# Second layer: the product of decay and state in an SBUF tile of its own, a later input between product and sum, and TensorE's spread of inputs ahead of most decays

## Chip, cores and metric

The kernel runs on one core of a Trainium2 chip. The metric is the device time of one execution, in microseconds (us), from a few executions of the same program. Everything is float32. Engines are named as in the profile: PE (TensorE; PEld are its weight loads), DVE (VectorE), ACT (ScalarE), POOL (GpSimd), SP (SyncE, which issues the DMAs). An instruction that is said to wait stands in its engine's queue, and everything behind it in that queue waits too.

## What is computed

Sixteen images of 128 x 56 x 56 go through two layers. Layer 0 (a depthwise convolution, window attention with routing, a depthwise 5 x 5 convolution and an MLP) isn't touched by the change. Layer 1 is a 3 x 3 convolution, a small state-space scan over eight tokens of 16 channels for every pixel, a group norm, a SiLU and a residual. The change is in the scan:

```
dA = jnp.exp(dt[..., None] * A)
dBx = dt[..., None] * Bm[:, :, None, :] * xc[..., None]

def step(h, inp):
    a, b, c = inp
    h = a * h + b
    return (h, jnp.sum(h * c[:, None, :], axis=-1))
```

The state h has 32 x 16 elements for each of 16 x 56 x 56 sequences, and eight tokens l = 0 to 7 follow each other.

## The kernel before

Layer 0 runs first, image by image; layer 1 follows from about 3.2 ms on and takes the rest. Its work is cut into 112 groups (16 images, seven blocks of 448 pixels each). A group goes through 14 steps, k = 0 to 13, in the loop at the end of `layer1` (L1284). A state of one token is a tile of 128 partitions x 4 x 448 elements; each step treats one half of it (`jp` = 0 or 1, two of the four slices, 896 elements per partition), so that two steps make one token, and the token of step k is l = 1 + k // 2.

Each engine runs its instructions in the order of the program text: `_chain` ties every instruction of the stage to the one before it on the same engine. What a step issues, in this order:

- `advance` (DVE): the product of decay and former state for step k. For l < 7 it is written in place over the decay in PSUM (L1001); for l = 7, whose input is accounted for elsewhere, it goes straight to the state's tile (L999).
- other DVE parts of the step (for k > 0): `collect` at k = 3 and 12 (L1032), `statistics` at k = 9 and 10 (L1080).
- `complete` (DVE, L1006): the sum of the product and the input, written to the state's tile in SBUF. It exists for l < 7, that is in steps 0 to 11.
- `inject` (DVE, L991): the input of step k + 4, made from the spread input in PSUM and a broadcast gate, written to the tile of its state. It takes that tile from the tag `h`, which has four buffers.
- at k = 0 only, `direct_mul` (DVE, L960), two instructions.
- `decay` (PE, L973) for step k + 2: two small matmuls into a PSUM tile of the tag `a`, which has two buffers.
- `spread` (PE, L984) for step k + 5: two small matmuls into the PSUM tile `x`, which has one buffer.
- `decay_exp` (ACT, L976): the exponential of the decay, in place in PSUM.
- `weigh` (POOL, L1010) in odd steps: the whole state of a token times a gate, 1792 elements per partition, into `cst`.
- further PE and POOL parts of the step from `work` (L1153): on PE the sums over weighted states (`gather`, L1019), the convolution of the next image, projections and transposes; on POOL `gated` (L1035) at k = 4 and 13, `rate_sum` (L922 to L925, four instructions) at k = 6 and 8, `product` (L951) at k = 10, and `store` (L1126) at k = 2 in four of seven groups.

SP brings the gates of the groups by DMA and stores the results. DVE's sum and weighing are joined by a semaphore: `weigh` of a token waits for the `complete` of its second half. The sum also waits on a semaphore for the product in front of it, on its own engine.

Of the kernel before, what the change touches and what calls it, by code (L numbers as in the profile page):

```python
# [10 lines left out]
F32 = mybir.dt.float32  # L11
U32 = mybir.dt.uint32
AF = mybir.ActivationFunctionType
ALU = mybir.AluOpType
# [3 lines left out]
P = 128  # L18
# [5 lines left out]
BLK = 448  # L24
# [771 lines left out]
def layer1(ctx: ExitStack, tc: tile.TileContext, x1, t, out, conv):  # L796
# [15 lines left out]
    nc = tc.nc  # L812
# [3 lines left out]
    cst = ctx.enter_context(tc.tile_pool(name="l1c", bufs=1))  # L816
    w1 = ctx.enter_context(tc.tile_pool(name="l1w1", bufs=1))
    w2 = ctx.enter_context(tc.tile_pool(name="l1w2", bufs=2))
# [14 lines left out]
    vec = conv.vec  # L833
# [5 lines left out]


    for w, name in ((wx, "b_kx"), (wv, "b_dtw")):
        k = w1.tile(list(w.shape), F32, tag="fold", name=name)
        nc.sync.dma_start(k, t[name])
        nc.vector.tensor_mul(w, w, k)
    nc.scalar.activation(adec, adec, AF.Exp)
    nc.vector.scalar_tensor_tensor(adec, adec, -1.0, mask, ALU.mult, ALU.mult)
    dd = cst.tile([P, P], F32, tag="dd", name="dd")
    nc.vector.tensor_scalar_mul(dd, ident, d_w)
    eps = cst.tile([P, 1], F32, tag="eps1", name="eps1")
    nc.vector.memset(eps, GN_EPS)  # L850
    neg = cst.tile([P, 1], F32, tag="neg", name="neg")
    nc.vector.memset(neg, -1.0)

    y, tails = conv.y, conv.tails
    pq = [ps_q.tile([P, 512], F32, tag=f"q{k}", name=f"pq{k}") for k in range(2)]
# [11 lines left out]
    def own(jp):  # L867
        return slice(2 * jp, 2 * jp + 2)
# [86 lines left out]
        nc.tensor.matmul(pq[0][:, 0:BLK], lhsT=cbm, rhs=p["cb"], start=True, stop=True)  # L955

    def direct_mul(p):
        ud = p["ud"] = w2.tile([P, 2, BLK], F32, tag="ud", name=f"ud_{p['n']}")
        for h in range(2):
            nc.vector.scalar_tensor_tensor(  # L960
                ud[:, h, :], pq[0][:, 0:BLK], vec[:, 6 + h : 7 + h], p["dtx"][:, h, :], ALU.mult, ALU.mult
            )


# [3 lines left out]
    def decay(p, l, jp):  # L968
        h, l4 = divmod(l, 4)
        a = p["a", l, jp] = ps_a.tile([P, 2, 512], F32, tag="a", name=f"a_{p['n']}_{l}_{jp}")[:, :, 0:BLK]  # L970
        for k in range(2):
            rows = slice(32 * (2 * jp + k), 32 * (2 * jp + k) + 32)
            nc.tensor.matmul(a[:, k, :], lhsT=adec[rows, l4, :], rhs=p["dt"][rows, h, :], start=True, stop=True)  # L973

    def decay_exp(p, l, jp):
        nc.scalar.activation(p["a", l, jp], p["a", l, jp], AF.Exp)  # L976

    def spread(p, l, jp):

        h, l4 = divmod(l, 4)  # L980
        x = ps_x.tile([P, 2, 512], F32, tag="x", name=f"x_{p['n']}_{l}_{jp}")[:, :, 0:BLK]
        for k in range(2):
            rows = slice(32 * (2 * jp + k), 32 * (2 * jp + k) + 32)
            nc.tensor.matmul(x[:, k, :], lhsT=mask[rows, l4, :], rhs=p["dtx"][rows, h, :], start=True, stop=True)  # L984
        px["x"] = x

    def inject(p, l, jp):
        if jp == 0:
            p["h", l] = w4.tile([P, 4, BLK], F32, tag="h", name=f"h_{p['n']}_{l}")
        weight = p["gate", 0, l].unsqueeze(1).to_broadcast([P, 2, BLK])  # L990
        nc.vector.tensor_mul(p["h", l][:, own(jp), :], px["x"], weight)  # L991

    def advance(p, l, jp):

        a, before = p["a", l, jp], p["h", l - 1][:, own(jp), :]
        if l == 7:
            if jp == 0:
                p["h", l] = w4.tile([P, 4, BLK], F32, tag="h", name=f"h_{p['n']}_{l}")
            nc.vector.tensor_mul(p["h", l][:, own(jp), :], a, before)  # L999
        else:  # L1000
            nc.vector.tensor_mul(a, a, before)  # L1001

    def complete(p, l, jp):
        if l < 7:
            h = p["h", l][:, own(jp), :]
            nc.vector.tensor_add(h, p["a", l, jp], h)  # L1006

    def weigh(p, l):
        c = p["c", l] = w4.tile([P, 4, BLK], F32, tag="cst", name=f"cst_{p['n']}_{l}")
        nc.gpsimd.tensor_mul(c, p["h", l], p["gate", 1, l].unsqueeze(1).to_broadcast([P, 4, BLK]))  # L1010
# [18 lines left out]
    def collect(p, h):  # L1029
        if h == 0:  # L1030
            p["ym"] = w1.tile([P, 2, BLK], F32, tag="ym", name=f"ym_{p['n']}")
        nc.vector.tensor_add(p["ym"][:, h, :], pq[1][:, 0:BLK], p["ud"][:, h, :])  # L1032

    def gated(p, h):
        nc.gpsimd.tensor_mul(p["ym"][:, h, :], p["ym"][:, h, :], p["zs"][:, h, :])  # L1035
# [117 lines left out]
    def work(i, k):  # L1153
# [8 lines left out]
        if prev:  # L1162
            if k == 0:
                pe += [partial(gather, prev, 5), partial(gather, prev, 6)]
            if k == 1:
                pe.append(partial(gather, prev, 7))
            if k == 3:
                dve.append(partial(collect, prev, 1))
            if k == 4:
                pool.append(partial(gated, prev, 1))  # L1170
            if k in (5, 6):
                pe.append(partial(project_out, prev, k - 5))
            b = prev["b"]
            if prev["g"] % 2 and k in (9, 10):
                dve.append(partial(statistics, b, prev["g"] - 10 + k))
            if prev["g"] == NBLK - 1:
                if k == 9:
                    dve.append(partial(statistics, b, NBLK - 1))
                if k == 12 and b < NB - 1:
                    residual(b, 0)  # L1180
# [26 lines left out]
        if p:  # L1207
            if i == len(groups) - 1 and k in (4, 6):
                residual(p["b"], k // 2 - 2)
            if k == 0:  # L1210
                dve.append(partial(direct_mul, p))
            if k == 7:
                pe.append(partial(skip, p, 0))
            if k in (8, 9, 10):
                pe.append(partial(gather, p, k - 7))
            if k == 12:
                dve.append(partial(collect, p, 0))
            if k == 13:
                if nxt:
                    pe.append(partial(direct, nxt))  # L1220
                pe += [partial(skip, p, 1), partial(gather, p, 4)]
                pool.append(partial(gated, p, 0))
            if k in (2, 6):
                bring(p, 0, {2: (4, 5), 6: (6,)}[k])
            if k in (1, 5, 9):
                bring(p, 1, {1: (3, 4), 5: (5, 6), 9: (7,)}[k])
# [41 lines left out]
    def state_step(i, k):  # L1268

        i, k = i + k // 14, k % 14  # L1270
        return (groups[i], 1 + k // 2, k % 2) if i < len(groups) else None

    def input_step(i, k):
        i, k = i + k // 14, k % 14
        return (groups[i], k // 2, k % 2) if i < len(groups) else None
# [8 lines left out]
    for i in range(-2, len(groups) + 3):  # L1284
        for k in range(14):
            now = 0 <= i < len(groups)
            pe, dve, pool = work(i, k)
            inputs = input_step(i, k + 4) if now or (i == -1 and k >= 10) else None
            further = input_step(i, k + 5) if now or (i == -1 and k >= 9) else None
            decays = state_step(i, k + 2) if now or (i == -1 and k >= 12) else None  # L1290

            if now:
                advance(*state_step(i, k))
            for part in dve if k else ():
                part()
            if now:
                complete(*state_step(i, k))
            if inputs:
                inject(*inputs)
            for part in () if k else dve:  # L1300
                part()
            if decays:
                decay(*decays)
            if further:
                spread(*further)
            if decays:
                decay_exp(*decays)
            if now and k % 2:
                weigh(groups[i], 1 + k // 2)
            for part in pe + pool:  # L1310
                part()
# [3 lines left out]
@with_exitstack  # L1315
def network(ctx: ExitStack, tc: tile.TileContext, t, out):
    NB = out.shape[0]
    dram = ctx.enter_context(tc.tile_pool(name="dram", bufs=1, space=bass.MemoryType.DRAM))
    x1 = [dram.tile([P, HW], F32, tag=f"x1_{b}", name=f"x1_{b}") for b in range(NB)]
    conv = Convolution(tc.nc, ctx.enter_context(tc.tile_pool(name="conv", bufs=1)), t, x1)  # L1320
    layer0(tc, t["x"], t, x1, conv)
    layer1(tc, x1, t, out, conv)
# [27 lines left out]
```

## Time and profile before

| | |
|---|---|
| median of 3 runs | 8306.25 us (8298.19 to 8308.66) |
| the profiled execution | 8305.77 us, its span 8304.0 us |
| granted TensorE clock | 0.983 of full speed |
| DMA | 757.87 MB moved, mean 91 GB/s |
| layer 1, first to last sum (L1006) | starts at 3199.4 and 8270.0 us |

The page's shares are averages over two layers with different limits, so that layer 1 has to be read from stretches inside it. In a line of a group of instructions there stand: line, engine, operation, output and inputs by the program's names, their shapes, and the count; then the busy time in us and the mean of one in ns; then the idle time of the engine just before them and what ended most of it. In a timeline each line is the start in us, the duration in us, engine, line and operation. A stretch shows the busy time of PE, PEld, DVE, ACT and POOL with instruction counts, then the granted clock, the DMA share and GB/s.

### The profile page before, as it was taken

What the parts mean: (1) busy time and instruction counts of PE and PEld (TensorE: products, weight loads), DVE (VectorE), ACT (ScalarE), POOL (GpSimd) and SP (SyncE); (2) the same over time, 40 slices, a digit from 0 to 9 for tenths busy, and PEclk for the clock granted to TensorE, in tenths of its full rate; (3) what the DMA queues carried; (4) which work ended last, traced back from release to release, by engine and by line L of the source; (5) the groups of instructions that cost most, each with busy time, mean ns of one, the idle gap of its engine ahead of it and who ended that gap; (6) DMA issues with size and microseconds to landing.
All of it is one profiled execution on the core that took longest, in us unless ns stands there. A gap on an engine that the chain in (4) does not pass through costs nothing.

```text
span 8304.0 us, 151471 instructions
## 1 busy us (share of the span) xinstructions
PE 7835.1 (94%) x52860; PEld 3329.9 (40%) x52860; DVE 7736.9 (93%) x10346; ACT 5642.6 (68%) x10579; POOL 7054.9 (85%) x5692
## 2 busy tenths in 40 slices
PE   5999999999999998999999999999999999999998
PEld 3444444444444453333333333333333333333332
DVE  7999999999999976999999999999999999999998
ACT  4777777777777755666666666666666666666665
POOL 7888788888888725899989999999999989999997
PEclk8999999999999999999999999999999999999998
DMA  3333333333333323333333334334333343334333
GB/s 65 87 86 87 85 89 87 87 87 87 87 87 87 81 79 82 87 93 102 99 92 99 96 91 105 91 97 106 83 104 100 88 105 103 86 99 108 85 93 88
DMA packets 764584, 757.87 MB, mean 91 GB/s; under 512 B 188720, under 2 KB 663984, under 8 KB 761904
## 3 DMA queue, kind: packets, MB, share of 16 engines
q1 hardware_dynamic: 763824, 748.18, 34.9%
q8 instruction: 423, 6.93, 0.4%
q14 instruction: 337, 2.76, 0.1%
HBM read 439.61 MB, written 102.76 MB: 65 GB/s over the span
## 4 chain that ended last, share of the span: by engine, by line
PE 34%; DVE 24%; POOL 24%; issue 9%; ACT 9%; DMA 1%; SPq 0%; POOLq 0%; ACTq 0%; DVEq 0%
PE a L973 7%; DVE h L991 6%; DVE a L1001 5%; POOL cst L1010 5%; PE x L984 5%; POOL xh L315 5%; PE pq L1019 5%; PE pq L892 4%; POOL e L431 4%; DVE h L1006 4%; DVE lepe L512 3%; POOL tap L313 3%; POOL dtx L925 2%; PE pq L931 2%; DVE sst L415 2%
## 5 line engine op out<-in xcount | busy, mean ns | idle before, releaser
L1010 POOL TENSOR_TENSOR cst<-h,cb 128x1792 f32<-128x1792 f32 x784 | 3130.6, 4000 | 348.9 <-DVE h L1006 291.1
L976 ACT ACTIVATE a<-a 128x896 f32<-128x896 f32 x1568 | 1415.7, 903 | 1080.2 <-PE x L984 588.0
L991 DVE TENSOR_TENSOR h<-x,bb 128x896 f32<-128x896 f32 x1568 | 1697.5, 1083 | 96.6 <-PE x L984 58.2
L512 DVE SCALAR_TENSOR_TENSOR lepe<-vpad,lep,lepe 128x448 f32<-128x448 f32 x2688 | 1718.0, 678 | 0.5
L984 PE MATMUL x<-dtx,amask 32*128 32x448 f32 x6272 | 1626.4, 595 | 49.0 <-DVE h L991 38.5
L973 PE MATMUL a<-dt,adec 32*128 32x448 f32 x6272 | 1620.2, 593 | 53.7 <-DVE h L1006 49.9
L1006 DVE TENSOR_TENSOR h<-a,h 128x896 f32<-128x896 f32 x1344 | 1463.1, 1089 | 38.1
L1001 DVE TENSOR_TENSOR a<-a,h 128x896 f32<-128x896 f32 x1344 | 1465.7, 1091 | 26.7 <-ACT a L976 25.8
L431 POOL TENSOR_SCALAR e<-e,sst,zero 128x256 f32<-128x256 f32 x1568 | 861.1, 559 | 466.6 <-DVE sst L427 417.4
L421 ACT ACTIVATE e<-ps,sst 128x256 f32<-128x256 f32 x1568 | 728.6, 469 | 522.5 <-DVE sst L415 470.5
L973 PEld LDWEIGHTS a<-dt,adec 32*128 32x128 f32 x6272 | 474.5, 185 | 1066.5 <-DVE h L1006 501.4
L315 POOL TENSOR_TENSOR xh<-xh,tap 128x448 f32<-128x448 f32 x749 | 859.6, 1148 | 43.7
L184 PE MATMUL pq<-pad,conv 128*128 128x448 f32 x1890 | 834.8, 559 | 0.0
L1019 PE MATMUL pq<-cst,sel 128*32 128x448 f32 x6272 | 734.5, 553 | 0.8 <-POOL cst L1010 0.8
L415 DVE TENSOR_REDUCE sst<-ps 128x2 f32<-128x512 f32 x784 | 540.3, 689 | 107.9 <-PE ps L409 83.0
L146 ACT ACT_TABLE_LOAD x484 | 621.0, 1283 | 9.3 <-PEq L1341 0.7
L453 PE MATMUL ptt<-ident,e 128*128 128x128 f32 x3136 | 538.6, 283 | 93.5 <-POOL e L431 76.8
L984 PEld LDWEIGHTS x<-dtx,amask 32*128 32x128 f32 x6272 | 476.7, 185 | 365.9 <-DVE h L991 344.3
L409 PE MATMUL ps<-sel,q 32*64 32x256 f32 x6272 | 537.3, 411 | 53.2 <-ACT e L421 46.9
L313 POOL TENSOR_SCALAR tap<-pad,pos,zero 128x448 f32<-128x448 f32 x749 | 546.5, 730 | 35.7
L453 PEld LDWEIGHTS ptt<-ident,e 128*128 128x128 f32 x3136 | 366.6, 141 | 417.5 <-POOL e L431 237.0
L459 ACT COPY att<-ptt 128x512 f32<-128x512 f32 x784 | 458.7, 585 | 72.0 <-PE ptt L453 64.1
(175 smaller groups left out, 12040.7 us busy)
## 6 DMA issues: line engine op xcount, KB each, us to landing
sel<-kv SPq DMA_DIRECT2D x3136, 64.0 KB
bb<-db SPq DMA_DIRECT2D x336, 448.0 KB
cb<-dc SPq DMA_DIRECT2D x336, 448.0 KB
pad<-x SPq DMA_DIRECT2D x32, 784.0 KB
x<-r SPq DMA_DIRECT2D x112, 224.0 KB
pad<-x SPq DMA_DIRECT2D x16, 1568.0 KB
db<-bs SPq DMA_DIRECT2D x112, 224.0 KB
dc<-cs SPq DMA_DIRECT2D x112, 224.0 KB
```

Of the source, the lines that this page charges most:

```text
L315: nc.gpsimd.tensor_add(im["xh"][i], im["xh"][i], held["tap"])
L431: nc.gpsimd.tensor_scalar(e, e, im["st", w][:, 2, p : p + 1], zero, ALU.mult, ALU.add)
L453: nc.tensor.transpose(ptt[:, P * (2 * p + h) : P * (2 * p + h + 1)], e[:, h * P : (h + 1) * P], ident)
L512: nc.vector.scalar_tensor_tensor(out, src, lep[:, k : k + 1], acc, ALU.mult, ALU.add)
L973: nc.tensor.matmul(a[:, k, :], lhsT=adec[rows, l4, :], rhs=p["dt"][rows, h, :], start=True, stop=True)
L976: nc.scalar.activation(p["a", l, jp], p["a", l, jp], AF.Exp)
L984: nc.tensor.matmul(x[:, k, :], lhsT=mask[rows, l4, :], rhs=p["dtx"][rows, h, :], start=True, stop=True)
L991: nc.vector.tensor_mul(p["h", l][:, own(jp), :], px["x"], weight)
L1001: nc.vector.tensor_mul(a, a, before)
L1006: nc.vector.tensor_add(h, p["a", l, jp], h)
L1010: nc.gpsimd.tensor_mul(c, p["h", l], p["gate", 1, l].unsqueeze(1).to_broadcast([P, 4, BLK]))
L1019: nc.tensor.matmul(py[32 * j : 32 * j + 32], lhsT=sel[:, l4, :], rhs=p["c", l][:, j, :], start=False, stop=(l % 4 == 3), skip_group_check= ...
```

## The change

In words: `advance` for l < 7 writes its product to a new tile `m` in SBUF (one buffer) instead of over the decay in PSUM, and `complete` reads it there. In the step's order `inject` and the other DVE parts now stand between `advance` and `complete`. On PE the `spread` of a step is issued ahead of its `decay`, except in steps 2, 10 and 11. To make room, the tiles of `ud` are split in two, one of them with one buffer; two set-up tiles share the tag of `m`, and two constants share a tile.

```diff
     for w, name in ((wx, "b_kx"), (wv, "b_dtw")):
-        k = w1.tile(list(w.shape), F32, tag="fold", name=name)
+        k = w1.tile(list(w.shape), F32, tag="m", name=name)
...
-    eps = cst.tile([P, 1], F32, tag="eps1", name="eps1")
+    small = cst.tile([P, 2], F32, tag="small", name="small")
+    eps, neg = small[:, 0:1], small[:, 1:2]
     nc.vector.memset(eps, GN_EPS)
-    neg = cst.tile([P, 1], F32, tag="neg", name="neg")
     nc.vector.memset(neg, -1.0)
...
     def direct_mul(p):
-        ud = p["ud"] = w2.tile([P, 2, BLK], F32, tag="ud", name=f"ud_{p['n']}")
         for h in range(2):
+            ud = p["ud", h] = (w1, w2)[h].tile([P, BLK], F32, tag=f"ud{h}", name=f"ud{h}_{p['n']}")
             nc.vector.scalar_tensor_tensor(
-                ud[:, h, :], pq[0][:, 0:BLK], vec[:, 6 + h : 7 + h], p["dtx"][:, h, :], ALU.mult, ALU.mult
+                ud, pq[0][:, 0:BLK], vec[:, 6 + h : 7 + h], p["dtx"][:, h, :], ALU.mult, ALU.mult
             )
...
         else:
-            nc.vector.tensor_mul(a, a, before)
+            m = p["m", l, jp] = w1.tile([P, 2, BLK], F32, tag="m", name=f"m_{p['n']}_{l}_{jp}")
+            nc.vector.tensor_mul(m, a, before)
 
     def complete(p, l, jp):
         if l < 7:
             h = p["h", l][:, own(jp), :]
-            nc.vector.tensor_add(h, p["a", l, jp], h)
+            nc.vector.tensor_add(h, p["m", l, jp], h)
...
                 advance(*state_step(i, k))
             for part in dve if k else ():
                 part()
-            if now:
-                complete(*state_step(i, k))
             if inputs:
                 inject(*inputs)
             for part in () if k else dve:
                 part()
-            if decays:
+            if now:
+                complete(*state_step(i, k))
+
+            apart = k in (2, 10, 11)
+            if decays and apart:
                 decay(*decays)
             if further:
                 spread(*further)
             if decays:
+                if not apart:
+                    decay(*decays)
                 decay_exp(*decays)
             if now and k % 2:
                 weigh(groups[i], 1 + k // 2)
```

More of the change, by code (lines that the diff above doesn't have):

```diff
@@ L1031, in collect @@
             p["ym"] = w1.tile([P, 2, BLK], F32, tag="ym", name=f"ym_{p['n']}")
-        nc.vector.tensor_add(p["ym"][:, h, :], pq[1][:, 0:BLK], p["ud"][:, h, :])
+        nc.vector.tensor_add(p["ym"][:, h, :], pq[1][:, 0:BLK], p["ud", h])
     def gated(p, h):
```

## The prediction

> **What bounds the kernel now.** I read the page's busy shares first, then the busy times by stretch, then the costliest groups, then the order of instructions on single engines.
>
> ```profile
> PE 7835.1 (94%) x52860; PEld 3329.9 (40%) x52860; DVE 7736.9 (93%) x10346; ACT 5642.6 (68%) x10579; POOL 7054.9 (85%) x5692
> 4500.00:5000.00 500.00, 488.71 (x2568) 180.38 (x2571) 484.96 (x497) 337.72 (x473) 454.38 (x217) 0.99 0.36 94
> ```
>
> The second line is one stretch of layer 1, columns as PE, PEld, DVE, ACT, POOL: VectorE is busy for 97% of it, GpSimd for 91%. PE's 98% is pipelined time. VectorE sets the pace, and GpSimd has little to spare.
>
> ```profile
> L1010 POOL TENSOR_TENSOR cst<-h,cb 128x1792 f32<-128x1792 f32 x784 | 3130.6, 4000 | 348.9 <-DVE h L1006 291.1
> L991 DVE TENSOR_TENSOR h<-x,bb 128x896 f32<-128x896 f32 x1568 | 1697.5, 1083 | 96.6 <-PE x L984 58.2
> L1006 DVE TENSOR_TENSOR h<-a,h 128x896 f32<-128x896 f32 x1344 | 1463.1, 1089 | 38.1
> L1001 DVE TENSOR_TENSOR a<-a,h 128x896 f32<-128x896 f32 x1344 | 1465.7, 1091 | 26.7 <-ACT a L976 25.8
> ```
>
> Each of the 14 steps of a group has an input (L991) and a product; twelve of them also a sum (L1006). Every second step GpSimd weighs a whole state, 4.00 us in one instruction. All three VectorE instructions have one operand in PSUM. The sums start between 3199.4 and 8270.0 us, which is 111 groups and 11 of 14 steps: 45.3 us per group.
>
> ```profile
> 5024.16 1.08 DVE L991 TENSOR_TENSOR h<-x,bb 128x896 f32<-128x896 f32 x1
> 5025.16 1.09 DVE L1001 TENSOR_TENSOR a<-a,h 128x896 f32<-128x896 f32 x1
> 5026.28 1.09 DVE L1006 TENSOR_TENSOR h<-a,h 128x896 f32<-128x896 f32 x1
> 5027.29 1.08 DVE L991 TENSOR_TENSOR h<-x,bb 128x896 f32<-128x896 f32 x1
> ```
>
> Input to product is 1.00 us from start to start, product to sum 1.12, sum to input 1.01. The extra 0.12 to 0.13 is the sum waiting for the product in front of it. A gap of that kind stands in 1122 of the 1344 sums; behind the others a collect or a statistic already lies between.
>
> The last view decides. In layer 0 one VectorE instruction, L303, has two inputs in SBUF, beside a busy GpSimd:
>
> ```profile
> L303 DVE SCALAR_TENSOR_TENSOR xh<-pad,pos,xh x147: 668/680/1439, 19.8 to 2892.9; 128x448 f32<-128x448 f32 x147
> ...
> 1121.60 0.68 DVE L303 SCALAR_TENSOR_TENSOR xh<-pad,pos,xh 128x448 f32<-128x448 f32 x1
> ...
> 1176.26 1.35 DVE L303 SCALAR_TENSOR_TENSOR xh<-pad,pos,xh 128x448 f32<-128x448 f32 x1
> ```
>
> ```profile
> 1120.65 1.13 POOL L315 TENSOR_TENSOR xh<-xh,tap 128x448 f32<-128x448 f32 x1
> ...
> 1175.98 1.14 POOL L315 TENSOR_TENSOR xh<-xh,tap 128x448 f32<-128x448 f32 x1
> ...
> 688.39 1.37 POOL L315 TENSOR_TENSOR xh<-xh,tap 128x448 f32<-128x448 f32 x1
> ```
>
> Where GpSimd's L315 ends 0.18 us after the start of L303 (1121.78), L303 takes its 0.68. Where L315 runs on to 1177.12, L303 takes 1.35 and ends at 1177.61, 0.49 after it. L512, with its accumulator in PSUM, is never stretched (mean 678 ns). In turn, the L315 of 688.39 met an L303 (688.10 to 688.78) that was already reading, and took 1.37 instead of 1.14. 50 of the 147 L303 are stretched, and nearly all of these end 0.48 us after a GpSimd instruction.
>
> **What the Trainium skill says.** "SBUF — State Buffer", section "Who interferes with whom": a VectorE instruction with two SBUF inputs contends with a GpSimd instruction that reads SBUF, and the second one is blocked until the first has finished; with at most one SBUF input it doesn't contend. The trace agrees on both counts (L303, L512), for lengths of 448. "VectorE: DVE Perf Modes", section "The perf-mode tier table": fp32 tensor_tensor runs at one element per cycle from SBUF as from PSUM, so moving the product gains no rate; no row of before has a busy GpSimd beside such an instruction. Same page, "The DRAIN you can't avoid": a read after a write on the same engine needs a semaphore or an instruction between, which is the gap of 0.12 us.
>
> **The change part by part.**
> (1) An input between product and sum. It covers the gap: 1122 x 0.126 = 141 us at most, 1.26 us per group. It also delays each sum by one input, 1.0 us; GpSimd's weighing waits for that.
> (2) The product goes to `m` in SBUF. This frees the PSUM tile at the product instead of at the sum, so a decay may start earlier (501 us of PEld waits on L1006). PE and ACT are not the bound, so I take nothing for it. The sum now reads m and h, both in SBUF: it becomes an instruction like L303. There are 12 per group, beside seven weighings of 4.00 us and a dozen instructions of 1.14 us that all read SBUF.
> (3) Spread ahead of decay. Spread waits for the input, decay now for a product before it, so both can go together; behind them stand gather, rate and gate. With a longer step PE has more room: nothing. Were it bound, a decay would be late by one spread, about 1.0 us, less than the two steps it is issued ahead.
> (4) `ud` in two tiles, the shared tag of `m` and `fold`, eps and neg in one tile: set-up, or the same instructions. Nothing.
>
> The price of (2), from the layout of one group on the two queues. Constants: from the end of one sum to the moment at which the next needs GpSimd's reads to be over, 2 x 1.00 + 0.15 - 0.09 = 2.06 us (0.15: a 448-long L1032 takes 615, an 896-long L991 1083, so 896 elements stream in 0.93 to 0.94 and 0.15 is set-up; 0.09: the overlap of 1.09 and 1.00). A blocked sum ends 0.95 after GpSimd's instruction (0.48 for 448 and 0.47 for 448 more). A blocked GpSimd instruction ends its own length less 0.15 after the sum (688.78 to 689.76 is 0.98 for 1.14): 1.0 or 3.85. Unblocked, a weighing starts 0.15 after its sum. A collect between costs 0.53.
> Time zero is the end of the sum of step 3; "wants" is when it could begin to read.
> - Weighing 2 from 0.2 to 4.2; sum 4 wants 2.1, ends 5.1; gated to 6.1; sum 5 wants 7.2, ends 8.1.
> - Weighing 3 from 8.3 to 12.3; sum 6 ends 13.2. Two of the four rate_sum instructions to 14.2 and 15.4; sum 7 ends 16.35; the other two to 17.35 and 18.55; sum 8 (wants 18.4) ends 19.5.
> - Weighing 4 to 23.35; sum 9 ends 24.3. Again two of rate_sum to 26.5; sum 10 ends 27.45; two to 29.65; sum 11 ends 30.6.
> - Weighing 5 to 34.45, product (L951) to 35.55, weighing 6 to 39.5. VectorE does the steps 12 and 13 meanwhile, but the input of the next step 0 takes the buffer of h(6), which weighing 6 reads (tag h has four): it starts at 39.7. Then direct_mul 1.18, so sum 0 wants 42.0.
> - Weighing 7 from 39.5 to 43.5; sum 0 ends 44.4; gated to 45.4; sum 1 wants 46.5, ends 47.4.
> - Weighing 1 from 47.6 to 51.6; sum 2 ends 52.5; sum 3, with the collect of step 3, wants 55.1 and ends at 56.1, with GpSimd idle as at zero.
> So a group takes 56.1 us instead of 45.3. 112 x 10.8 = 1210; 8304.0 + 1210 = 9514 for the span, and the profiled execution is 1.8 us longer than its span (8305.77): 9515. The median of the runs is 0.5 above that execution, which changes nothing. The gain of (1) is inside the layout, as steps without the gap.
>
> Not seen in before: a contention at length 1792 and of tensor_tensor on VectorE, and who wins when both wait. Lower end: the 4 us instruction lets VectorE in earlier, and GpSimd is never idle. Then the shared reads add up: 7 x 4.00 + 8 x 1.14 + 1.14 + 2 x 1.14 + 60 x 1.85 / 112 = 41.5 for GpSimd, and 12 x (0.95 - 0.15) = 9.6: 51.1, +5.8 x 112 = 650, 8955. Upper end: a waiting sum loses twice per group to a further short instruction of 1.2 us: 58.5, 9784. I take the layout between them, since the trace shows whole-instruction blocking.
>
> **The rivals.**
> - Blocking for whole instructions, VectorE next at each end: 9515, in 9275 (one of the layout's four waits of some 2 us stays away: 2.1 x 112 = 240) to 9784.
> - Blocking in shorter pieces: 8955 to 9275. For it: the weighing has four rows of 448. Against: L303 waited for L315 to its end.
> - GpSimd wins at the boundaries: 9784 to 10050 (2.4 to 4.8 us more per group, two to four short instructions). Against: L303 got in behind one copy (L484) while the next was already waiting, at 59.0 us.
> - The other side: no contention for tensor_tensor, the waits go. 8304 - 141 - some 20 of the 58 us in which L991 waits for PE: about 8145. GpSimd's 41.5 of 44.0 us stay below the new pace. It decides from a mean wait per sum below 1.26 / 12 = 0.105 us. Against it: 27 to 28 of any 56 us are one of seven weighings, and no page excludes tensor_tensor.
>
> **How the numbers follow.** 0.71 for the layout, 0.15 for shorter pieces, 0.08 for the boundaries, 0.05 for the other side, 0.01 for a cancellation within 0.2%, which is about what a measurement of this kernel can tell from no change. The range reaches from 8955 to 9800 and holds the first two cases, 0.86. Faster 0.05, same 0.01, slower 0.94.
>
> **What would show it.** L1006 should read h<-m,h with a mean of some 1.9 us (the waits of the layout sum to 10 us in 12 sums) and four of twelve near 3; L1001 and L991 unchanged at 1.09; the sum 1.00 behind an input; L1010 somewhat above 4.00, and the rate_sum rows above 1.14; PE's share of the layer 1 stretches down; layer 0 as before up to 3.2 ms. I am wrong if L1006 stays at 1.09 beside a running L1010. If it is stretched but the time is far from 9515, the layout failed, not the mechanism.

## The result, and the profile after

The changed kernel takes 9725.51 us (median of 4 runs, 9725.18 to 9728.64) against 8303.99 us: 1.171 times as long, 95% interval 1.169 to 1.173. The profiled execution has a span of 9723.5 us, 1419.5 more than before.

The engines' shares on the page after, and one stretch of layer 1 (columns as before):

```profile
PE 8002.5 (82%) x52860; PEld 3321.1 (34%) x52860; DVE 8698.6 (89%) x10346; ACT 5651.6 (58%) x10579; POOL 7737.0 (80%) x5692
...
4500.00:5000.00 500.00, 395.67 (x2004) 140.52 (x2007) 455.38 (x389) 263.36 (x370) 415.66 (x172) 0.91 0.29 74
```

VectorE did 389 instructions in a stretch in which it did 497 before, and was busy for almost as long: its instructions have become longer. GpSimd's busy time grew by 682 us with the same instructions. Which ones, the costliest groups show:

```profile
L1011 POOL TENSOR_TENSOR cst<-h,cb 128x1792 f32<-128x1792 f32 x784 | 3267.1, 4173 | 1155.1 <-PE a L973 1036.8
L1007 DVE TENSOR_TENSOR h<-m,h 128x896 f32<-128x896 f32 x1344 | 2424.4, 1804 | 0.0
L991 DVE TENSOR_TENSOR h<-x,bb 128x896 f32<-128x896 f32 x1568 | 1695.8, 1082 | 497.9 <-PE a L973 327.5
L1002 DVE TENSOR_TENSOR m<-a,h 128x896 f32<-128x896 f32 x1344 | 1466.2, 1091 | 132.4 <-DVE h L1007 2.3
L922 POOL TENSOR_TENSOR u<-u,e 128x448 f32<-128x448 f32 x224 | 443.1, 1978 | 72.8 <-ACT u L916 72.8
```

The sum (L1007, L1006 before) went from 1089 to 1804 ns; product and input, which have one SBUF input each, kept 1091 and 1082. On GpSimd the first instruction of rate_sum (L922) went from 1.14 to 1.98 us. So 961 of the 1420 us are longer sums. The idle time ahead of the input grew by 401 us (96.6 to 497.9; ahead of the step 0 input alone from 0.17 to 1.95 us per group) and that ahead of the product by 106 (26.7 to 132.4), while the sum's own 38 is gone.

VectorE and then GpSimd in the same microseconds of a group, in the timeline after (start, duration, engine, line):

```profile
5020.83 1.08 DVE L1007 TENSOR_TENSOR h<-m,h 128x896 f32<-128x896 f32 x1
5022.02 1.09 DVE L1002 TENSOR_TENSOR m<-a,h 128x896 f32<-128x896 f32 x1
5023.03 1.08 DVE L991 TENSOR_TENSOR h<-x,bb 128x896 f32<-128x896 f32 x1
5024.02 3.06 DVE L1007 TENSOR_TENSOR h<-m,h 128x896 f32<-128x896 f32 x1
5027.18 1.09 DVE L1002 TENSOR_TENSOR m<-a,h 128x896 f32<-128x896 f32 x1
```

```profile
5022.14 3.99 POOL L1011 TENSOR_TENSOR cst<-h,cb 128x1792 f32<-128x1792 f32 x1 [2.43 <-PE a L973]
5026.09 1.99 POOL L922 TENSOR_TENSOR u<-u,e 128x448 f32<-128x448 f32 x1
5028.16 1.13 POOL L923 TENSOR_TENSOR ln<-ln,u 128x448 f32<-128x448 f32 x1
```

The sum that starts at 5024.02 finds the weighing running. It ends at 5027.08, 0.95 us after the weighing's end (5026.13). L922, issued at 5026.09, is blocked in its turn and ends at 5028.08, 1.00 after the sum. The input at 5023.03 lay inside the same weighing and kept its 1.08. In the whole trace 604 of the 1344 sums are longer than 1.2 us, and every one of them ends 0.945 to 0.958 us after a GpSimd instruction, having waited for exactly one. Where a weighing starts 0.05 to 0.07 us after a sum, as 172 do, the sum keeps its 1.08 and the weighing takes 4.84 to 4.88 us: the later one waits.

A second thing is to be seen in the first fence: a product starts 0.11 us after the end of the sum in front of it (5021.91, 5022.02), where in the kernel before an input started 0.08 before that end. A product into `m` waits until the sum that reads `m` has finished.

### The profile page after: what moved, and what is told of

Read it like the earlier page. It is cut to its first block, busy times and chain, and to the rows that moved or that the text cites. A ratio compares the mean times of both kernels' runs of the same rounds, so it can differ in the third digit from the quotient of the medians.

```text
span 9723.5 us, 153034 instructions
## 1 busy us (share of the span) xinstructions
PE 8002.5 (82%) x52860; PEld 3321.1 (34%) x52860; DVE 8698.6 (89%) x10346; ACT 5651.6 (58%) x10579; POOL 7737.0 (80%) x5692
## 4 chain that ended last, share of the span: by engine, by line
DVE 40%; POOL 28%; PE 14%; issue 11%; ACT 5%; DMA 0%; SPq 0%; DVEq 0%; POOLq 0%; ACTq 0%
DVE h L1007 15%; DVE h L991 11%; POOL cst L1011 8%; DVE m L1002 6%; PE x L984 5%; POOL xh L315 4%; POOL e L431 4%; PE pq L892 3%; POOL tap L313 3%; POOL u L922 3%; DVE lepe L512 2%; POOL dt L924 2%; POOL ln L923 1%; POOL dtx L925 1%; DVE sst L415 1%
## 5 line engine op out<-in xcount | busy, mean ns | idle before, releaser
L1011 POOL TENSOR_TENSOR cst<-h,cb 128x1792 f32<-128x1792 f32 x784 | 3267.1, 4173 | 1155.1 <-PE a L973 1036.8
L984 PE MATMUL x<-dtx,amask 32*128 32x448 f32 x6272 | 1761.4, 640 | 1285.3 <-DVE h L991 1265.8
L1007 DVE TENSOR_TENSOR h<-m,h 128x896 f32<-128x896 f32 x1344 | 2424.4, 1804 | 0.0
L991 DVE TENSOR_TENSOR h<-x,bb 128x896 f32<-128x896 f32 x1568 | 1695.8, 1082 | 497.9 <-PE a L973 327.5
L973 PE MATMUL a<-dt,adec 32*128 32x448 f32 x6272 | 1756.3, 638 | 71.7 <-DVE m L1002 71.7
L1002 DVE TENSOR_TENSOR m<-a,h 128x896 f32<-128x896 f32 x1344 | 1466.2, 1091 | 132.4 <-DVE h L1007 2.3
L984 PEld LDWEIGHTS x<-dtx,amask 32*128 32x128 f32 x6272 | 519.0, 201 | 2362.7 <-DVE h L991 1993.5
L973 PEld LDWEIGHTS a<-dt,adec 32*128 32x128 f32 x6272 | 515.5, 201 | 314.3 <-DVE m L1002 290.9
L922 POOL TENSOR_TENSOR u<-u,e 128x448 f32<-128x448 f32 x224 | 443.1, 1978 | 72.8 <-ACT u L916 72.8
```

The costliest lines, as they stand in the source:

```text
L1002: nc.vector.tensor_mul(m, a, before)
L1007: nc.vector.tensor_add(h, p["m", l, jp], h)
```

## The experiments

Periods per group below are means from the start of a group's first product to that of the next; "waits" are what the sums take above 1.08 us, per group.

### The product back in PSUM, the new order kept

```diff
-            m = p["m", l, jp] = w1.tile([P, 2, BLK], F32, tag="m", name=f"m_{p['n']}_{l}_{jp}")
-            nc.vector.tensor_mul(m, a, before)
+            nc.vector.tensor_mul(a, a, before)
...
-            nc.vector.tensor_add(h, p["m", l, jp], h)
+            nc.vector.tensor_add(h, p["a", l, jp], h)
```

> The changed kernel with the product back in place over the decay in PSUM; the new order on VectorE and TensorE stays. Theory (the sum's two SBUF inputs contend with GpSimd's reads): sums back at 1.08 to 1.09 us each with none stretched, product to sum without the 0.12 us gap; 8304 - 141 = 8163 us, in 8080 to 8304. Rival (the order costs: the sum and with it the weighing come one input later, spread before decay delays TensorE): most of the loss stays, over 9000 us.

8586.82 us, 1.034 times the kernel before (1.032 to 1.035); the period is 47.96 us against 45.31 before and 58.06 after. Its lines:

```profile
L991 DVE TENSOR_TENSOR h<-x,bb 128x896 f32<-128x896 f32 x1568 | 1696.6, 1082 | 431.0 <-PE a L973 234.5
...
L1006 DVE TENSOR_TENSOR h<-a,h 128x896 f32<-128x896 f32 x1344 | 1449.2, 1078 | 0.0
```

No sum is stretched, beside a GpSimd that is as busy as ever. 1139 of the 1422 us go with the second SBUF input. But the order by itself does not gain 141 us; in place it loses 280, which neither theory had. The input now has 431 us of idle time before it, most of it put down to TensorE. By steps, from product to product: steps 1, 2 and 5 are shorter (3.13 to 3.00), as meant; step 0 goes from 4.52 to 5.76, step 6 from 3.40 to 3.96, step 8 from 3.17 to 3.73.

### Only the tile, in the order of before

The loop is that of before; `m` stays.

> The kernel of before in its order on VectorE and TensorE, with only the product moved to the SBUF tile m. Theory: the loss stays, since the sum has two SBUF inputs: mean of a sum 1.6 to 1.9 us, 9300 to 9750 us; the gap of 0.12 us between product and sum is back, that of 0.19 us between sum and next product is gone, because an input lies between. Rival (order): 8304 to 8450 us.

9647.59 us, 1.162 times (1.159 to 1.164), period 57.4. The line of its sums:

```profile
L1007 DVE TENSOR_TENSOR h<-m,h 128x896 f32<-128x896 f32 x1344 | 2665.8, 1983 | 38.6
```

The tile alone brings nearly the whole loss; the waits are 10.8 us per group instead of 8.7. The mean of a sum is above the expected 1.9, the time inside the range. The gaps are as expected: product to sum 1.11 us from start to start, with no extra wait ahead of a product. The parts do not add up (280 + 1341 is more than 1422): what waits for one thing does not wait for the other.

### GpSimd writes only

```diff
-        nc.gpsimd.tensor_mul(c, p["h", l], p["gate", 1, l].unsqueeze(1).to_broadcast([P, 4, BLK]))
+        for _ in range(2):
+            nc.gpsimd.memset(c, 0.0)
```

> The changed kernel; the weighing by the gate is left out, and GpSimd fills cst with zeros by two memsets instead (some 3.5 us by the 711 ns of a memset of 720), which read nothing. Theory (contention of reads): no sum beside a memset is stretched; only those beside rate_sum, gated, product and store, which still read, wait, at most 1.2 us each: mean of a sum at most 1.3 us instead of 1.80, and 8350 to 8700 us. Rival (any busy GpSimd holds VectorE up): sums beside the memsets wait for 1.5 us and more, mean over 1.5 us, over 9000 us.

The weighing's product is missing from this kernel; GpSimd only fills its tile with zeros. 8740.99 us (one run), the mean of a sum 1188 ns, the period 49.2. The timeline of VectorE, then of GpSimd:

```profile
5004.72 1.08 DVE L1007 TENSOR_TENSOR h<-m,h 128x896 f32<-128x896 f32 x1
5005.91 1.09 DVE L1002 TENSOR_TENSOR m<-a,h 128x896 f32<-128x896 f32 x1
5006.92 1.08 DVE L991 TENSOR_TENSOR h<-x,bb 128x896 f32<-128x896 f32 x1
5007.91 2.03 DVE L1007 TENSOR_TENSOR h<-m,h 128x896 f32<-128x896 f32 x1
...
5015.24 1.08 DVE L1007 TENSOR_TENSOR h<-m,h 128x896 f32<-128x896 f32 x1
```

```profile
5004.65 3.24 POOL L1012 MEMSET cst<- 128x1792 f32 x2
5007.86 1.14 POOL L922 TENSOR_TENSOR u<-u,e 128x448 f32<-128x448 f32 x1
...
5014.08 3.23 POOL L1012 MEMSET cst<- 128x1792 f32 x2
```

The sum at 5015.24 lies inside the time of two memsets and takes 1.08; the one at 5007.91 meets an L922 of 1.14 us and takes 2.03. Over the trace 401 sums found a memset running when they would begin to read, and none of them is stretched; all 315 that are stretched met an instruction that reads. It is the reading, not a busy GpSimd. The time is 41 us above the expected range. It lets one estimate what the rest of the change is worth: less the 143 us of remaining waits this would be 8598, still above the kernel before, with 329 us of idle time ahead of the input (97 before) and the gap of 0.19 behind the sums.

### The weighing in two halves

```diff
-        nc.gpsimd.tensor_mul(c, p["h", l], p["gate", 1, l].unsqueeze(1).to_broadcast([P, 4, BLK]))
+        for jp in range(2):
+            nc.gpsimd.tensor_mul(
+                c[:, own(jp), :], p["h", l][:, own(jp), :], p["gate", 1, l].unsqueeze(1).to_broadcast([P, 2, BLK])
+            )
```

> The changed kernel with every weighing of 1792 elements as two instructions of 896 (some 2.05 us each). Theory (held for the whole instruction, VectorE next at each end): the sums of steps 2, 4 and 6 get in between the halves, so their waits of 1.9 us fall to 0.2 to 0.4; mean of a sum 1.2 to 1.4 us, 8950 to 9300 us although GpSimd has 784 instructions more. Rival (what counts is the time for which GpSimd reads, in whatever pieces): no change or slower, 9650 to 9850 us.

9279.68 us, 1.117 times (1.115 to 1.119): 446 us less than the changed kernel, with 784 more instructions on GpSimd and the same elements read.

```profile
L1007 DVE TENSOR_TENSOR h<-m,h 128x896 f32<-128x896 f32 x1344 | 1931.3, 1437 | 0.0
```

The sums of steps 2, 4 and 6 fell from 2.96, 2.98 and 3.03 us to 1.09, 1.08 and 1.08: they get in between the halves. Some sums elsewhere wait more (steps 3 and 5 from 1.08 to 1.59 and 1.93), and that of step 9 still takes 2.39. So the total of what GpSimd reads does not set the price, and the rival falls. But the split also moves the reads: the first half needs only the sum of the even step, and for the tokens of steps 1, 3 and 5 it starts 3.0 us before the end of the odd sum, where the whole weighing started 0.1 to 0.2 us after it. How much of the 446 us comes from shorter instructions and how much from that earlier start is not separated.

### Every second sum

`m` in even steps only, or in odd steps only; the other product in place.

```diff
-            m = p["m", l, jp] = w1.tile([P, 2, BLK], F32, tag="m", name=f"m_{p['n']}_{l}_{jp}")
+            m = p["m", l, jp] = a
+            if jp == 0:
+                m = p["m", l, jp] = w1.tile([P, 2, BLK], F32, tag="m", name=f"m_{p['n']}_{l}_{jp}")
```

> The changed kernel with the product in the tile m in even steps only (in odd ones in place in PSUM). Theory (a sum waits where a weighing of 4 us is running; that starts behind an odd sum, so it is the even sums that meet it): even sums keep waits of about 2 us in steps 2, 4, 6; 4 to 7 us per group in all, 8950 to 9400 us. Behind a sum from m the next product goes to PSUM, so that the gap of 0.19 us is gone (1.00 from start to start if not stretched). Rival (every sum with two SBUF inputs costs about the same): as much as with odd steps alone, 8950 to 9150 us both.

> The same with the product in m in odd steps only. Theory: the odd sums come when the last weighing is over, except in steps 9 and 11, where GpSimd lags behind rate_sum; 0.5 to 2.5 us per group of waits, 8450 to 8800 us, clearly faster than with even steps alone. Rival: the same as with even steps alone, 8950 to 9150 us.

Even steps: 9724.14 us, 1.171 times (1.167 to 1.174). Odd steps: 9071.41, 1.092 times (1.089 to 1.095). The line of the sums from `m` in each, even first:

```profile
L1009 DVE TENSOR_TENSOR h<-m,h 128x896 f32<-128x896 f32 x672 | 2158.9, 3213 | 0.0
```

```profile
L1009 DVE TENSOR_TENSOR h<-m,h 128x896 f32<-128x896 f32 x672 | 1250.4, 1861 | 0.0
```

The order of the two is as the theory had it, the sizes are not: both are dearer than expected. With half as many such sums the even kernel loses as much as the change, since its sums in steps 8 and 10 now wait 3.5 and 2.9 us. In the odd one the waits are 4.7 us per group where 0.5 to 2.5 were expected, 2.8 of them in step 11. In the changed kernel it is the sum of step 9 that is long (2.31 us), and that of step 8 hardly is (1.15); how the queues shift against each other there was read from the means by step alone. The number of such instructions says little; where each falls beside the 4 us instructions says more. Behind an unstretched sum from `m` the next product, into PSUM, starts 1.00 us after the sum's start instead of 1.19: the gap belongs to the single buffer of `m`.

### TensorE's order

Decay ahead of spread in all steps, once with the product in PSUM, once with `m`.

```diff
-            apart = k in (2, 10, 11)
-            if decays and apart:
+            if decays:
                 decay(*decays)
             if further:
                 spread(*further)
             if decays:
-                if not apart:
-                    decay(*decays)
                 decay_exp(*decays)
```

> Product in place in PSUM, the new order on VectorE, TensorE's order as before (decay ahead of spread in all steps). Theory A (the loss of 280 us in the run with the new order on both engines comes from spread standing ahead of a decay that waits for the later sum): 8200 to 8400 us. Theory B (it comes from the later sum itself, since in place the decay's PSUM tile is free only after it): 8500 us or more.

> The changed kernel with TensorE's order as before, product in SBUF. Theory (TensorE has room beside stretched sums, and its order is worth little): 9725 us within 100. Rival (TensorE's order carries a part of the loss with m in SBUF too): 9500 us or less.

In PSUM 8564.40 us, 1.031 times (1.028 to 1.034), 22 less than with the new order; with `m` 9778.19, 1.177 times (1.174 to 1.181), 53 more. So TensorE's new order gains a half per cent with `m`. Without `m` the difference is not clear of noise (1.028 to 1.034 against 1.032 to 1.035). With TensorE's order as before 261 us of loss remain, so the 280 come from VectorE's order (theory B). Waits of TensorE's weight loads between 3500 and 8000 us, in the kernel before and in this one in PSUM (total us, times, longest):

```profile
PEld a L973 <- DVE h L1006: 426.3, 552, 1.2
```

```profile
PEld a L973 <- DVE h L1006: 1409.4, 1121, 3.2
```

In place the decay's tile is free only after the sum. The sum comes one input later, and the decay's weight loads wait for it twice as often and 1.26 us in the mean instead of 0.77, with spread and everything else on TensorE behind them.

### The new order in a few steps only

In place, with the change's order in steps 0 to 5, and in steps 0 to 2.

```diff
+            early = k < 6
-            if now:
+            if now and not early:
                 complete(*state_step(i, k))
             if inputs:
                 inject(*inputs)
             for part in () if k else dve:
                 part()
+            if now and early:
+                complete(*state_step(i, k))
```

> Product in place in PSUM as before; the change's order on both engines in steps 0 to 5, the order of before in steps 6 to 13. Theory (the gap of 0.126 us can be filled where TensorE has room, and the new order loses in the steps with the next image's convolution): five gaps less per group, step 3 having had a collect there already: 8304 - 5 x 0.126 x 112 = 8233 us, 8200 to 8290. Rival (the later sum costs as much as the gap wherever it is): 8300 us or more.

> Product in place in PSUM as before; the change's order in steps 0 to 2 only, the order of before in steps 3 to 13. Theory (three gaps filled, no loss where the two orders meet, since step 3 has a collect between and no convolution): 8304 - 3 x 0.126 x 112 = 8262 us, 8245 to 8300. Rival (where the orders meet something is late again, as with six steps): 8310 us or more.

8409.92 us, 1.012 times (1.010 to 1.014), and 8373.94, 1.0085 times (1.0072 to 1.0099): both rivals by their numbers, but with a reason that neither named. In the second kernel steps 1 and 2 last 2.99 and 3.00 instead of 3.13, as meant; step 0 lasts 5.24 instead of 4.52. VectorE's waits between 3500 and 8000 us there, and the same wait before:

```profile
DVE h L991 <- POOL cst L1010: 68.2, 111, 0.7
```

```profile
DVE h L991 <- POOL cst L1010: 16.5, 32, 0.6
```

The input issued in step 0 takes the buffer of h(6). In 79 of the 112 groups of the second kernel it waits for the weighing of h(6) and starts about 0.03 us after its end (57 us of idle time in the whole trace), and in 32 groups about 0.15 us after the end of its spread (49 us, for which the profile names no releaser). Before, 19 us of idle time stand ahead of this input, all put down to spread; the waits of the last line are those of step 12. Before, sum 0 ran ahead of this input; in the new order sum 0 and the work behind it stand behind its wait. Where steps 0 to 5 have the new order, step 6 loses as well (3.96 against 3.40). A version with the new order in steps 1, 2 and 4 alone would keep gains of 0.14, 0.13 and 0.06 us per group, an estimated 37 us if nothing else lengthens; that one was not tried, and none of the kernels here beats the one before.

### TensorE kept busy at the group's end

In the changed kernel, TensorE stands idle for 4.3 us at the end of a group and then runs slower. Ahead of the spread of step 12 a number of small matmuls went into columns of a PSUM tile that nothing reads.

```diff
+            if now and k == 12:
+                for _ in range(30):
+                    nc.tensor.matmul(
+                        groups[i]["all", 7, 1][:, 0, BLK:512], lhsT=ident, rhs=ident[:, 0:64], start=True, stop=True
+                    )
             if further:
                 spread(*further)
```

> The changed kernel with 30 small matmuls (64 columns, into columns of a decay's PSUM tile that nothing reads) ahead of the spread of step 12, where TensorE stands idle for 4.3 us in the changed kernel and then runs at a granted clock of 0.5. Theory (the slow clock behind that idle time makes spread and projection late at the end of a group, and the inputs of steps 13 and 0 wait for them): clock of layer 1 back over 0.95, the distance of the inputs of steps 12 and 13 from 3.05 to about 2.2 us, 1 to 2.2 us less per group: 9480 to 9615 us. Rival (those inputs wait for something else): 9700 us or more.

> As with the 30 small matmuls, but six: the 30 (60 instructions) took 12.9 us where 4.3 were free, and were late themselves; six are some 2.6 us at full clock. Theory (slow clock at the group's end): the distance of the inputs of steps 12 and 13 falls from 3.05 to 2.2 to 2.6 us, that of 13 and 0 from 4.05 to about 2.8, 1 to 2 us less per group: 9500 to 9615 us. Rival (the clock there is not what those inputs wait for): 9690 us or more.

With 30: 9943.10 us, 1.197 times (1.195 to 1.199). With six: 9723.06, 1.171 times (1.168 to 1.174), the changed kernel's time. TensorE in one group of each, and the inputs of the first kernel over the whole trace (L993 here, L991 before, with 497.9 us of idle time in the changed kernel):

```profile
5043.80 12.90 PE L1311 MATMUL a<-ident 128*128 128x64 f32 x60
```

```profile
5046.77 1.45 PE L1311 MATMUL a<-ident 128*128 128x64 f32 x12
5051.29 1.12 PE L986 MATMUL x<-dtx,amask 32*128 32x448 f32 x2 [3.06 <-DVE h L993]
```

```profile
L993 DVE TENSOR_TENSOR h<-x,bb 128x896 f32<-128x896 f32 x1568 | 1695.6, 1081 | 269.4 <-POOL cst L1013 144.2
```

The 12.9 us belong to a group in which the clock was at half. In 91 of the 112 groups the 60 instructions took 6.8 us, at full clock, and in 21 some 13. Either is more than the 4.3 us that were free. The product of step 13 reads the tile into which they write and waited 423 us for them, so step 12 grew from 3.86 to 7.64 us. But behind them the clock was up: 0.91 of full speed in the mean of step 13, where the changed kernel has 0.50, and steps 13 and 0 fell from 3.05 and 6.61 us to 2.14 and 5.61. The inputs of 13 and 0 came 2.81 us apart instead of 4.04. The idle time ahead of these two inputs fell from 2.9 to 0.9 us per group. The total time is the rival's, but the waits went as the theory had it.

The six took 1.45 us (the expected 2.6 had come from the 12.9) and left 3.06 us idle. They did not lift the clock (0.57 in step 13), and the steps stayed at 2.83 and 6.78.

The run with the product back in PSUM and the new order on both engines has both clocks in one execution. In 60 groups TensorE had its full clock between the product of step 13 and the next input of step 0, and the two inputs had 0.75 us of idle time before them; in 24 groups the clock was under 0.6, and they had 3.80. In the changed kernel it is 2.9 us, and no group has the full clock there. So the slow clock goes with most of these waits. From these figures it is worth an estimated 2 us of the 58.06 per group; a run that lifts the clock without adding work to the queue was not made.

## Why the prediction was right

It said 9515 us in 8955 to 9800; it is 9725.5. The likeliest case was the one that came, and its points compare as follows.

- **The sum blocked for whole instructions.** Shown: stretched beside the weighing, not beside memsets, not with a PSUM operand; with the weighing in halves the sums of steps 2, 4 and 6 get in. Predicted for the sum were a mean of 1.9 us and four of twelve near 3; it is 1.80, and steps 2, 4 and 6 stand at 2.96 to 3.03, steps 9 and 11 at 2.31 and 2.24. The layout's waits add up to 10.1 us per group, the trace has 8.7. The layout has 1.5 us in step 0 (0.2 measured), and 0.15 in step 11 (1.2 measured).
- **Who is next.** VectorE. At 506 of the 604 boundaries GpSimd's next instruction stood ready as well, and VectorE came first at each; at the other 98 GpSimd had nothing for over 3 us. The rival in which GpSimd wins and the one of shorter pieces fall with it. A blocked GpSimd instruction of 1.14 us ends 1.00 after the sum, as taken from layer 0.
- **The constant that was wrong.** "0.09: the overlap of 1.09 and 1.00" was taken from before, where an input follows the sum. A product into `m` follows now and starts 0.11 after the sum's end: 1.19 from start to start instead of 1.00. Eleven times per group that is 2.1 us, or some 230 us in all; the period came out 58.06 instead of 56.1. Part of the 2.1 shortens the waits that follow (those of 2.1 us became 1.9), so that the two don't simply add to the layout.
- **"(1) covers the gap: 1.26 us per group."** It does, but the gap reappears behind the sum for want of a second buffer, 2.07 us against 1.26. A second buffer of `m` was not tried; the change had to make room for the first.
- **"(3) Spread ahead of decay: nothing."** Within 53 us of 9725, and for the better. "A decay may start earlier: I take nothing for it" is tested by no run alone, and it does not seem to be nothing in the new order: in place steps 6 and 8 grow to 3.96 and 3.73 us, since the decay's tile then waits for the later sum; with `m`, and without the weighing's reads, they last 3.29 and 3.23. The gap behind the sum takes that back.
- **The rival on the other side** (8145 if nothing contended) would by these numbers have failed too. With the weighing's reads gone the changed kernel takes 8741, of which 143 are remaining waits. Contention is not all that stood against the gain: the gap behind the sum and inputs that wait for TensorE at the end of a group take it back.
- **The group's end, where the total came out near by luck.** By its own constants the layout has 3.7 us of idle time there, all ahead of step 0's input, for weighing 6. The trace has 4.2 us: 1.3 ahead of step 12's input, which takes the buffer of h(5) and waits for weighing 5, and 1.0 and 1.95 ahead of the inputs of steps 13 and 0, put down to TensorE. The layout missed the first ("VectorE does the steps 12 and 13 meanwhile") and left TensorE out ("PE has more room: nothing"). Step 0's wait belongs to VectorE's new order: it is 1.29 us with the product back in PSUM and 1.77 without the weighing's reads, but 0.17 both before and with the tile alone, where sum 0 stands ahead of that input. Most of the waits for TensorE go with its slow clock. Over the whole group, too, waits that were too long (10.1 against 8.7) stood against terms that were missing (the gap behind the sum, TensorE), so that 9515 lies nearer to 9725 than its parts do.

## What to carry to other kernels

Before moving an operand from PSUM to SBUF, count the SBUF inputs of the VectorE instruction that reads it, and look at what GpSimd reads beside it: with two inputs VectorE waits for the end of whatever GpSimd is reading, so a 1 us instruction can cost 3 us next to one of 4 us. Look in the trace for a row of such an instruction whose maximum is far over its median: it shows the price of one such meeting before any experiment. Then count the buffers of the new tile: with a single one the next writer waits for its reader (here 1.19 us from start to start instead of 1.00).

## What the runs showed that was not expected

TensorE's clock followed the stalls. Stretches at a group's end in the changed kernel, with the clock in the column before the last two:

```profile
5038.00:5044.00 6.00, 5.72 (x26) 1.95 (x28) 5.79 (x7) 2.50 (x5) 5.76 (x5) 1.00 0.34 115
...
5050.00:5051.00 1.00, 1.00 (x8) 0.17 (x4) 0.59 (x1) 0.00 (x0) 1.00 (x1) 0.50 0.00 0
5051.00:5052.00 1.00, 1.00 (x5) 0.50 (x2) 0.44 (x1) 0.38 (x1) 1.00 (x1) 0.50 0.00 0
...
5055.00:5057.00 2.00, 2.00 (x12) 0.70 (x8) 1.17 (x2) 1.98 (x3) 2.00 (x1) 1.00 0.94 274
```

TensorE stood idle for 4.3 us in front of the spread of step 12 and ran at half its clock until 5054.6. The four matmul instructions of L892 took 3.32 us there; in the kernel before, with the clock at 0.99, 1.77 (changed kernel, then before):

```profile
5049.65 1.12 PE L984 MATMUL x<-dtx,amask 32*128 32x448 f32 x2 [4.34 <-DVE h L991]
...
5051.46 3.32 PE L892 MATMUL pq<-seq,wx 128*128 128x448 f32 x4
```

```profile
5009.94 1.77 PE L892 MATMUL pq<-seq,wx 128*128 128x448 f32 x4
```

This comes in every group: the mean clock of step 13 over the trace is 0.50, and the commonest slow stretches last 3.41 and 6.83 us, about one of each in the 58 us of a group. The Trainium skill, "TensorE: Matmul & The Clock Gate", section "Part 1: The HAM clock gate", says that the half rate comes after at least one idle window of about 3.4 us. The trace agrees with a window of that length, since the commonest stretches of one clock last 3.41, 6.83, 17.07 and 30.72 us, all multiples of 3.41. It does not bear out an idle time of that length as the condition: in the run with the product back in PSUM and the new order on both engines, 67 slow stretches lie in layer 1, and in the 6.8 us ahead of each the longest idle time of TensorE was 1.6 us at most. What is enough to bring the slow clock stays open. A stall on VectorE can thus make TensorE slower as well as later.
